# Layer 2's graph: each group of gathered edges waits for the gathers of two groups behind it

## The chip, the cores and the metric

The kernel runs on one core of one Trainium2 chip. The metric is the device time of one execution in microseconds (us). A core has five engines that run side by side, each through a queue of instructions of its own: TensorE (PE in the profile; its weight loads are PEld), VectorE (DVE), ScalarE (ACT), GpSimd (POOL) and SyncE (SP). An engine takes its queue in order. An instruction that has to wait for another engine or for a DMA holds up everything behind it in its queue.

## What is computed

The network has four layers over 4608 tokens (2 images of 48 x 48) of 256 channels: a bidirectional selective scan, linear attention with a convolution, attention followed by a graph-routed mixture of experts, and sigmoid attention followed by a second mixture of experts. The change lies in the graph of layer 2, which scores each token for four experts by attention over 1048576 edges. The core of the reference:

```python
h = (x_flat @ W_gat).reshape(M, HEADS, NUM_EXPERTS)
loops = jnp.arange(M, dtype=edge_index.dtype)
src = jnp.concatenate([edge_index[0], loops])
dst = jnp.concatenate([edge_index[1], loops])
a_src = (h * att_src).sum(-1)
a_dst = (h * att_dst).sum(-1)
e = jax.nn.leaky_relu(a_src[src] + a_dst[dst], negative_slope=0.2)
e_max = jax.ops.segment_max(e, dst, num_segments=M)
ee = jnp.exp(e - e_max[dst])
denom = jax.ops.segment_sum(ee, dst, num_segments=M)
alpha = ee / (denom[dst] + 1e-16)
msg = h[src] * alpha[:, :, None]
agg = jax.ops.segment_sum(msg, dst, num_segments=M).reshape(M, HEADS * NUM_EXPERTS) + b_gat
...
for ei in range(NUM_EXPERTS):
    g = jnp.where(topk_i == ei, w, 0.0).sum(-1)
    hh = jax.nn.gelu(x @ W1[ei] + b1[ei], approximate=False)
    out = out + g[..., None] * (hh @ W2[ei] + b2[ei])
```

The drawn edges point at up to 65536 nodes, of which 4608 exist here; an index out of range is clamped for a source and dropped for a target. Nearly all edges therefore have the last node as their source.

## The kernel before

While layers 0 and 1 run, the edges are packed into sortable keys, and each partition keeps the first ones. Edges whose source is the last node only have to be counted by target. The others are few: `edges.oth` holds 64 of them for each of the 128 partitions, one column of 128 edges at a time.

`graph_scores` handles both kinds in one block between two loops with a run-time count (lines 1131 and 1402), which no instruction crosses. In it three streams of work meet:

- The counts (`count_last`): 32 groups of 32 columns. For each, DVE builds a one-hot of the low index bits (`ol`, L1103, 128 x 4096 in bf16) and one of the high bits (`oh`, L1107), and PE multiplies them in 32 small matmuls (L1109) into one accumulator. Both one-hots have two buffers.
- The pieces (`beside[1]`): four pieces of the experts' first pass, which need no graph: matmuls `ph` (L1511), Gelu on ACT (L1515), matmuls `po` (L1526), an addition on ACT (L1530). `behind_gathers` interleaves three steps of these with each count.
- The edges (`add_edges`): eight groups of eight columns. For each column POOL issues two indirect DMAs, one that gathers the source's row into `gs` (L1207) and one for the target's row into `gd` (L1211): 128 gathers, all issued ahead of the counts in the program's text, each group into buffers of its own (eight of them). Once a group's rows are there, DVE builds the high one-hot (`oh`, L1220, which needs no gather), adds the two attention terms (`e`, L1225), applies the leaky ReLU (L1226) and subtracts the bound (L1227); ACT takes the exponential (L1228); DVE forms the message rows (L1229), and for each column a low one-hot (`ol`, L1237) and the outer product of rows and high one-hot (`wide`, L1239, 128 x 720). PE multiplies these in two matmuls per column (L1243) into `fp`. The tiles `e`, `rows` and the edges' `oh` have two buffers, `ol` and `wide` four.

The order in each engine's queue is not the order of the text. When the program is built, a scheduler plays it through with durations of its own: whenever an engine is free in that plan, it gets the instruction that comes first in the text among those whose operands are ready and whose buffers are free. The queues that come out are then fixed. The text has the counts and pieces ahead of the groups of edges, so a group's instruction gets onto DVE among the counts only where the plan finds DVE free. On the chip each instruction waits, by semaphores, for what it really needs.

After the block, layer 2 goes on with further pieces on PE, while DVE turns `acc` into the gate values `g`; then the late pieces and layer 3 follow.

Of the kernel before, what the change touches and what calls it, by code (L numbers as in the profile page):

```python
# [98 lines left out]
def bc(ap, shape, axis):  # L99

    return ap.unsqueeze(axis).to_broadcast(shape)
# [1070 lines left out]
def decode(nc, wp, bits, sidx, didx):  # L1172

    nc.vector.tensor_scalar(sidx, bits, 13, 0x1FFF, ALU.logical_shift_right, ALU.bitwise_and)
    nc.vector.tensor_scalar(sidx, sidx, -1.0, float(T - 1), ALU.mult, ALU.add)
    none = wp.tile(list(bits.shape), F32, tag="none", name="none")
    nc.vector.tensor_scalar(none, bits, 0.0, float(T), ALU.is_equal, ALU.mult)
    nc.vector.tensor_single_scalar(didx, bits, 0x1FFF, ALU.bitwise_and)
    nc.vector.tensor_tensor(didx, didx, none, ALU.add)


def add_edges(E, pools, keys, t_src, t_dst, lo_row, hi_row, fp, beside=None):


    nc = E.nc
    H, X, F, HI = 4, 4, 20, NT
    GQ = 8
    ip, cp = pools
    n = keys.shape[1]
    bits = keys.bitcast(I32)  # L1190
    sidx = ip.tile([P, n], I32, tag="sidx", name="sidx")
    didx = ip.tile([P, n], I32, tag="didx", name="didx")
    decode(nc, ip, bits, sidx, didx)
    part_i = ip.tile([P, n], I32, tag="part_i", name="part_i")
    lo = ip.tile([P, n], F32, tag="lo", name="lo")
    hi = ip.tile([P, n], F32, tag="hi", name="hi")
    nc.vector.tensor_single_scalar(part_i, didx, P - 1, ALU.bitwise_and)
    nc.vector.tensor_copy(lo, part_i)
    nc.vector.tensor_single_scalar(part_i, didx, 7, ALU.logical_shift_right)
    nc.vector.tensor_copy(hi, part_i)  # L1200
    got = []
    for q in range(n // GQ):
        gs = cp.tile([P, GQ, F], F32, tag="gs", name="gs")
        gd = cp.tile([P, GQ, 2 * H], F32, tag="gd", name="gd")
        for j in range(GQ):
            o = q * GQ + j
            nc.gpsimd.indirect_dma_start(  # L1207
                out=gs[:, j, :], out_offset=None, in_=t_src[:, :],
                in_offset=bass.IndirectOffsetOnAxis(ap=sidx[:, o : o + 1], axis=0),
            )  # L1210
            nc.gpsimd.indirect_dma_start(  # L1211
                out=gd[:, j, :], out_offset=None, in_=t_dst[:, :],
                in_offset=bass.IndirectOffsetOnAxis(ap=didx[:, o : o + 1], axis=0),
            )
        got.append((gs, gd))
    if beside is not None:
        beside()
    for q, (gs, gd) in enumerate(got):
        oh = cp.tile([P, GQ, HI], F32, tag="oh", name="oh", bufs=2)
        nc.vector.tensor_tensor(  # L1220
            oh, bc(hi[:, q * GQ : (q + 1) * GQ], [P, GQ, HI], 2), bc(hi_row, [P, GQ, HI], 1), ALU.is_equal
        )
        e = cp.tile([P, GQ, H], F32, tag="e", name="e", bufs=2)
        rows = cp.tile([P, GQ, F], F32, tag="rows", name="rows", bufs=2)
        nc.vector.tensor_tensor(e, gs[:, :, 0:H], gd[:, :, 0:H], ALU.add)  # L1225
        nc.vector.scalar_tensor_tensor(e, e, 0.2, e, ALU.mult, ALU.max)  # L1226
        nc.vector.tensor_tensor(e, e, gd[:, :, H:], ALU.subtract)  # L1227
        nc.scalar.activation(rows[:, :, H * X :], e, AF.Exp)  # L1228
        nc.vector.tensor_tensor(  # L1229
            rows[:, :, : H * X].rearrange("p i (h e) -> p i h e", h=H),  # L1230
            gs[:, :, H:].rearrange("p i (h e) -> p i h e", h=H),
            bc(rows[:, :, H * X :], [P, GQ, H, X], 3), ALU.mult,
        )
        for j in range(GQ):
            o = q * GQ + j
            ol = cp.tile([P, P], F32, tag="ol", name="ol", bufs=4)
            nc.vector.tensor_scalar(ol, lo_row, lo[:, o : o + 1], None, ALU.is_equal)  # L1237
            wide = cp.tile([P, HI, F], F32, tag="wide", name="wide", bufs=4)
            nc.vector.tensor_tensor(  # L1239
                wide, bc(oh[:, j, :], [P, HI, F], 2), bc(rows[:, j, :], [P, HI, F], 1), ALU.mult  # L1240
            )
            for z in range(2):
                nc.tensor.matmul(  # L1243
                    fp[z], lhsT=ol,
                    rhs=wide[:, z * HI // 2 : (z + 1) * HI // 2, :].rearrange("p i f -> p (i f)"),
                    start=o == 0, stop=o == n - 1,
                )


def graph_scores(E, xn, g, edges, beside, n_beside):  # L1250
# [8 lines left out]
    nc, tc, p = E.nc, E.tc, E.p  # L1259
    H, X, F, HI = 4, 4, 20, NT  # L1260
    DUMMY = T

    with ExitStack() as ctx:
        keep = ctx.enter_context(tc.tile_pool(name="gkeep", bufs=1))
        acc = keep.tile([P, HI, F], F32, name="acc")
        t_src = E.dram.tile([T, F], F32, name="t_src")
        t_dst = E.dram.tile([T + 1, 2 * H], F32, name="t_dst")
        lo_row = edges.lo_row
        hi_row = keep.tile([P, HI], F32, name="hi_row")
# [115 lines left out]
        with (  # L1385
            tc.tile_pool(name="goi", bufs=1) as ip,
            tc.tile_pool(name="goc", bufs=8) as cp,
            tc.tile_pool(name="gops", bufs=1, space=PSUM) as ps,
        ):
            fp = [ps.tile([P, HI // 2 * F], F32, name=f"fp{z}") for z in range(2)]  # L1390
            add_edges(E, (ip, cp), edges.oth, t_src, t_dst, lo_row, hi_row, fp, behind_gathers)
            for z in range(2):
                nc.vector.tensor_tensor(halves[z], halves[z], fp[z], ALU.add)

# [2 lines left out]
        with (  # L1397
            tc.tile_pool(name="gloop", bufs=1) as ip,
            tc.tile_pool(name="gcol", bufs=2) as cp,
            tc.tile_pool(name="gps", bufs=1, space=PSUM) as ps,  # L1400
        ):
            with tc.For_i(0, n_rounds, 1):
                rest = ip.tile([P, edges.NR], F32, tag="rest", name="rest")
                nc.sync.dma_start(rest, edges.rest_d[:, :])
                k8 = ip.tile([P, NP * 8], F32, tag="k8", name="k8")
                for j in range(NP):
                    part = rest[:, j * 1024 : (j + 1) * 1024]
                    nc.vector.max(k8[:, j * 8 : (j + 1) * 8], part)
                    nc.vector.match_replace(part, k8[:, j * 8 : (j + 1) * 8], part, 0.0)
                nc.sync.dma_start(edges.rest_d[:, :], rest)  # L1410
                fp = [ps.tile([P, HI // 2 * F], F32, tag=f"fp{z}", name=f"fp{z}") for z in range(2)]
                add_edges(E, (ip, cp), k8, t_src, t_dst, lo_row, hi_row, fp)
                for z in range(2):
                    nc.vector.tensor_tensor(halves[z], halves[z], fp[z], ALU.add)
# [57 lines left out]
def layer2_ffn(ctx, E, edges):  # L1472
# [61 lines left out]
    def pieces(a, b):  # L1534
        for c in range(a, b):
            yield from early(c)

    graph_scores(
        E, xn, g, edges, (pieces(0, AHEAD), pieces(AHEAD, BESIDE)), (BESIDE - AHEAD) * NX * (FT + 2)
    )  # L1540
# [592 lines left out]
```

## Time and profile before

| | |
|---|---|
| Runs | 5334.69, 5338.10, 5339.48 us; median 5338.1 us |
| Profiled execution | 5298.49 us, span 5296.7 us, mean granted TensorE clock 0.964 |
| Busy share of the span | PE 90%, DVE 66%, POOL 46%, ACT 45% |
| Counts, first and last L1103 | 3531.7 and 3756.3 us from the start of the span |
| Gathers, first and last issued | 3538.7 and 3814.5 us |
| Edges' matmuls (L1243), main run | 3777.05 to 3855.5 us |

The profile is of one execution. A timeline row has the start, the duration, the engine, the line, the operation, what it writes and reads, how many instructions are merged into it, and in brackets how long the engine stood idle just before it and what ended that. A gather's row on POOL shows how long POOL worked on issuing it; the data land later. Times below are counted from the start of the span.

### The profile page before, as it was taken

To read this page: it belongs to the slowest core of one execution; us is meant where nothing else is said; L and a number is where in the kernel's file an instruction comes from. 1 tells how busy PE (TensorE), PEld (TensorE's weight loads), DVE (VectorE), ACT (ScalarE), POOL (GpSimd) and SP (SyncE) were. 2 spreads that over 40 slices of the span, in tenths; PEclk is the share of its full clock that TensorE was granted. 3 is DMA by queue.
4 is the path that set the end of the run, shared out by engine and by line. 5 is a ranking of instruction groups with operands and counts; after the bars stand their busy time and mean duration, and the time that the engine had idled before them with its cause. 6 is when DMAs were issued, how large, how long until landed. Compare 5 with 4: busy or idle time off the path is not lost. (4 is left out here: it accounts for less than half of the span.)

```text
span 5296.7 us, 47498 instructions
## 1 busy us (share of the span) xinstructions
PE 4765.0 (90%) x15282; PEld 2642.2 (50%) x15282; DVE 3472.5 (66%) x5366; ACT 2395.3 (45%) x5021; POOL 2416.0 (46%) x1323
## 2 busy tenths in 40 slices
PE   7888888888888888877999999999999999999897
PEld 3444344444444434433555555556655555555676
DVE  4999988889888878889999544546724410211344
ACT  5767766765766766762222323422133222222221
POOL 2888887788888788886000000028612100000331
PEclk8999999999999999999999999999989999999898
DMA  4454454444544344443110000111121100000422
GB/s 155 167 173 172 169 177 159 167 173 165 173 150 161 138 162 152 162 152 135 36 44 32 6 16 1 38 33 28 19 96 48 48 3 9 7 9 6 85 84 97
DMA packets 187427, 504.63 MB, mean 95 GB/s; under 512 B 33591, under 2 KB 106683, under 8 KB 186908
## 3 DMA queue, kind: packets, MB, share of 16 engines
q1 hardware_dynamic: 178460, 488.74, 26.9%
q0 software_dynamic: 8704, 12.73, 1.6%
q8 instruction: 123, 2.02, 0.2%
q14 instruction: 140, 1.15, 0.1%
HBM read 425.88 MB, written 75.51 MB: 95 GB/s over the span
## 5 line engine op out<-in xcount | busy, mean ns | idle before, releaser
L512 PE MATMUL yp<-hc,ident 128*128 128x384 f32 x3072 | 1185.8, 517 | 206.3 <-DVE hc L558 166.1
L527 POOL TENSOR_TENSOR db<-dtu,bb 128x1536 f32<-128x1536 f32 x384 | 1322.9, 3445 | 53.5 <-DVE hs L553 13.5
L512 PEld LDWEIGHTS yp<-hc,ident 128*128 128x128 f32 x3072 | 573.4, 197 | 764.5 <-DVE hc L558 317.7
L558 POOL TENSOR_TENSOR hc<-ho,cc 128x384 f32<-128x384 f32 x576 | 587.9, 1028 | 243.6 <-DVE ho L553 103.1
L558 DVE TENSOR_TENSOR hc<-hs,cc 128x384 f32<-128x384 f32 x960 | 499.9, 538 | 82.5 <-PE yp L512 81.3
L544 ACT ACTIVATE hs<-dt,negab 128x384 f32<-128x384 f32 x768 | 435.2, 581 | 94.6 <-DVE hc L558 44.1
L544 ACT ACTIVATE hs<-dt,negaf 128x384 f32<-128x384 f32 x768 | 434.5, 581 | 67.3 <-DVE hc L558 32.6
L550 DVE TENSOR_TENSOR_SCAN hs<-hs,state,db 128x384 f32<-128x384 f32 x400 | 395.3, 1008 | 33.9 <-POOL db L527 21.5
L553 DVE TENSOR_TENSOR_SCAN hs<-hs,state,db 128x384 f32<-128x384 f32 x400 | 393.3, 1005 | 34.6 <-POOL db L527 16.1
L1938 POOL DMA_INDIRECT xe<-xt_d,token x48 | 47.4, 987 | 752.5 <-issue 713.1
L311 PE MATMUL mm<-xw,w_cv 128*128 128x384 f32 x768 | 287.5, 517 | 56.6 <-ACT xs L315 17.9
L1873 PE MATMUL po<-at,xtok 128*128 128x384 f32 x864 | 329.5, 506 | 8.2 <-ACT at L1871 8.1
L1864 PE MATMUL sp<-qT,xn 128*128 128x384 f32 x864 | 317.2, 486 | 0.0
L1871 ACT ACTIVATE at<-sp 128x384 f32<-128x384 f32 x216 | 104.8, 491 | 467.2 <-PE sp L1864 467.1
L1511 PE MATMUL ph<-xn,w 128*128 128x384 f32 x768 | 288.9, 519 | 17.7 <-ACT hid L1515 6.0
L1069 POOL PARTITION_ALL_REDUCE most<-most x1 | 0.4, 381 | 629.5 <-PE tp L939 629.5
L800 PE MATMUL pf<-t,wfc 128*128 128x384 f32 x768 | 256.0, 488 | 3.5 <-ACT hid L804 2.7
L819 PE MATMUL po<-hid,wfc 128*128 128x384 f32 x768 | 253.7, 486 | 0.0
L553 DVE TENSOR_TENSOR_SCAN ho<-hs,state,db 128x384 f32<-128x384 f32 x240 | 239.2, 997 | 14.4 <-ACT hs L544 14.3
L550 DVE TENSOR_TENSOR_SCAN ho<-hs,state,db 128x384 f32<-128x384 f32 x240 | 239.0, 996 | 8.7 <-ACT hs L544 8.7
L560 ACT COPY state<-hs 128x1 f32<-128x1 f32 x800 | 117.6, 155 | 277.5 <-DVE hc L558 274.6
L1515 ACT ACTIVATE hid<-ph,vec 128x384 f32<-128x384 f32 x192 | 110.6, 581 | 292.8 <-PE ph L1511 259.2
(465 smaller groups left out, 8022.8 us busy)
## 6 DMA issues: line engine op xcount, KB each, us to landing
bb<-bcd SPq DMA_DIRECT2D x192, 768.0 KB, 4.2
cc<-bcd SPq DMA_DIRECT2D x192, 768.0 KB, 4.1
xw<-xi_d SPq DMA_DIRECT2D x24, 774.0 KB, 5.8
w<-in_m_w SPq DMA_DIRECT2D x16, 1024.0 KB, 5.8
y_d<-y SPq DMA_DIRECT2D x32, 384.0 KB, 2.3
ye<-y_d SPq DMA_DIRECT2D x32, 384.0 KB, 3.4
xi_d<-xz SPq DMA_DIRECT2D x48, 192.0 KB, 2.3
z_d<-xz SPq DMA_DIRECT2D x48, 192.0 KB, 3.2
```

Of the source, the lines that this page charges most:

```text
L311: nc.tensor.matmul(px, lhsT=w_cv[b, s][:, d * 4 + k, :], rhs=xw[:, d, o : o + W], start=k == 0, stop=k == 3,)
L512: nc.tensor.matmul(yp[d], lhsT=E.ident, rhs=hc, start=False, stop=summed[d] == NS)
L527: nc.gpsimd.tensor_tensor(db, bc(dtu[:, d, :], [P, GN, W], 1), bb, ALU.mult)
L544: nc.scalar.activation(hs, dt[:, d, :], AF.Exp, scale=nega[s][:, d * NS + n : d * NS + n + 1])
L550: nc.vector.tensor_tensor_scan(to, hs, db[:, j], init, ALU.mult, ALU.add)
L553: nc.vector.tensor_tensor_scan(to[:, ::-1], hs[:, ::-1], db[:, j, ::-1], init, ALU.mult, ALU.add)
L558: (nc.gpsimd if on_pool else nc.vector).tensor_tensor(hc, to, cc[:, j, :], ALU.mult)
L800: nc.tensor.matmul(pf, lhsT=wfc1[:, k, f * P : (f + 1) * P], rhs=t1[:, k, :], start=k == 0, stop=k == 1,)
L819: nc.tensor.matmul(po[m], lhsT=wfc2[:, f, m * P : (m + 1) * P], rhs=hid[:, i, :], start=f == 0, stop=f == 15,)
L1511: nc.tensor.matmul(ph, lhsT=w1[:, e, k, f * P : (f + 1) * P], rhs=xn[:, k, c * W : (c + 1) * W], start=k == 0, stop=k == 1,)
L1864: nc.tensor.matmul(sp, lhsT=xn[:, k, t0 + i * P : t0 + (i + 1) * P], rhs=qT[:, k, c * W : (c + 1) * W], start=k == 0, stop=k == 1,)
L1873: nc.tensor.matmul(po[m], lhsT=xtok[:, i, m * P : (m + 1) * P], rhs=at, start=i == 0, stop=i == MT - 1,)
```

## The change

Each group's `e` gets a first write ahead of its real one. It copies one column of a later group's `gd`, the last column that is gathered there, into a part of `e`, which L1225 then overwrites. The later group is the one two further on, or the last group where there is none. The value is of no use; the copy, and so everything of the group that uses `e`, has to wait for that later gather. Only the call in `graph_scores` asks for it; the second call, in the loop over further edges, keeps the default of 0 and is unchanged.

```diff
-def add_edges(E, pools, keys, t_src, t_dst, lo_row, hi_row, fp, beside=None):
+def add_edges(E, pools, keys, t_src, t_dst, lo_row, hi_row, fp, beside=None, behind=0):
...
         e = cp.tile([P, GQ, H], F32, tag="e", name="e", bufs=2)
         rows = cp.tile([P, GQ, F], F32, tag="rows", name="rows", bufs=2)
+        if behind:
+
+            later = got[min(q + behind, len(got) - 1)][1]
+            nc.vector.tensor_copy(e[:, GQ - 1, H - 1 :], later[:, GQ - 1, 0:1])
         nc.vector.tensor_tensor(e, gs[:, :, 0:H], gd[:, :, 0:H], ALU.add)
         nc.vector.scalar_tensor_tensor(e, e, 0.2, e, ALU.mult, ALU.max)
...
-            add_edges(E, (ip, cp), edges.oth, t_src, t_dst, lo_row, hi_row, fp, behind_gathers)
+            add_edges(E, (ip, cp), edges.oth, t_src, t_dst, lo_row, hi_row, fp, behind_gathers, 2)
```

## The prediction

> **What bounds the kernel now.** I read the page first, for the engine that fills the span, then the timelines of VectorE (DVE), GpSimd (POOL) and TensorE (PE) over the graph of layer 2, and the waits there.
>
> ```profile
> span 5296.7 us, 47498 instructions
> PE 4765.0 (90%) x15282; PEld 2642.2 (50%) x15282; DVE 3472.5 (66%) x5366; ACT 2395.3 (45%) x5021; POOL 2416.0 (46%) x1323
> ```
>
> PE is busy 90% of the span, so a microsecond counts where PE loses it. The graph's block runs from 3525 us to 3856 us. PE first does counts and expert pieces, then the edges' matmuls (L1243):
>
> ```profile
> 3672.52 5.49 PE L1511 MATMUL ph<-xn,w 128*128 128x384 f32 x8 [5.78 <-ACT hid L1515]
> ...
> 3702.61 2.19 PE L1109 MATMUL cp<-oh,ol 128*128 128x36 bf16 x32 [4.91 <-DVE oh L1107]
> ...
> 3777.05 40.70 PE L1243 MATMUL fp<-wide,ol 128*128 128x360 f32 x134
> 3818.89 36.57 PE L1243 MATMUL fp<-wide,ol 128*128 128x360 f32 x120 [1.15 <-DVE wide L1239]
> 3855.30 1.45 PE L1511 MATMUL ph<-xn,w 128*128 128x384 f32 x4
> ```
>
> In 3603 to 3855 PE waits three times: 5.78 us for ACT, 4.91 us for a count's one-hot on DVE, 1.15 us for the last group. From 3777.05 the 64 edge columns run back to back for 78.25 us, 9.78 us a group. Behind them PE goes straight on (L1511), so the whole kernel moves by what the end of L1243 moves. The cause of the waits is in DVE's queue:
>
> ```profile
> 3628.92 0.45 DVE L1220 TENSOR_TENSOR oh<-hi,hi_row 128x288 f32<-128x288 f32 x1
> 3629.29 0.19 DVE L1225 TENSOR_TENSOR e<-gs,gd 128x32 f32<-128x32 f32 x1
> ...
> 3659.57 0.19 DVE L1225 TENSOR_TENSOR e<-gs,gd 128x32 f32<-128x32 f32 x1
> 3669.79 0.19 DVE L1225 TENSOR_TENSOR e<-gs,gd 128x32 f32<-128x32 f32 x1 [10.03 <-DMA gd<-t_dst,didx]
> ...
> 3680.44 0.18 DVE L1227 TENSOR_TENSOR e<-e,gd 128x32 f32<-128x32 f32 x1
> 3696.91 0.19 DVE L1225 TENSOR_TENSOR e<-gs,gd 128x32 f32<-128x32 f32 x1 [16.28 <-DMA gd<-t_dst,didx]
> ...
> 3817.63 0.19 DVE L1225 TENSOR_TENSOR e<-gs,gd 128x32 f32<-128x32 f32 x1 [3.25 <-DMA gd<-t_dst,didx]
> ```
>
> L1225 is a group's first use of its gathers. Groups 0 to 3 stand between the counts (L1103, 32 of them): group 0 behind count 16, groups 1 and 2 behind count 20, group 3 behind count 22; groups 4 to 7 come after the counts. I call these slots 16, 20 and 22. Groups 2 and 3 come before their gathers have landed, and the queue stands 10.03 and 16.28 us. The queue's order was fixed at build, by a plan that thought those gathers done. ACT stands in the same way, since its exp (L1228) is queued ahead of the pieces' Gelu:
>
> ```profile
> 3670.35 0.23 ACT L1228 ACTIVATE rows<-e 128x32 f32<-128x32 f32 x1 [9.04 <-DVE e L1227]
> ```
>
> The reader should see that these are the waits behind PE's 5.78 and 4.91 us. POOL says when gathers are done:
>
> ```profile
> 3559.48 0.94 POOL L1207 DMA_INDIRECT gs<-t_src,sidx  x1 [0.30 <-issue]
> 3560.73 4.37 POOL L1211 DMA_INDIRECT gd<-t_dst,didx  x1 [0.30 <-issue]
> ...
> 3662.47 0.94 POOL L1211 DMA_INDIRECT gd<-t_dst,didx  x1 [0.30 <-issue]
> ...
> 3814.49 0.94 POOL L1211 DMA_INDIRECT gd<-t_dst,didx  x1 [0.30 <-issue]
> ```
>
> A gather is 0.94 us and 0.30 us to the next, 1.25 us. One issued under a count's L1103 (4.42 us) lasts as long as that. Group 2's 48 gathers were issued 129.7 us after the first one (3538.7), with 19 counts in between: (129.7 - 48 x 1.25)/19 = 3.66 us per count. Group 3's 64 took 156.7 us with 21 counts: 3.65. So n gathers with k counts take 1.25n + 3.65k, and the last of them has landed 1.5 to 2.2 us later (3695.44 to 3696.91, 3815.43 to 3817.63); I take 2.2.
>
> **The change part by part.** It removes nothing and moves no DMA; POOL's and SP's queues keep their order. It adds eight copies of 128x1 on DVE. The nearest row is the 128x1 scalar operation at L924, 145 ns: 8 x 0.15 = 1.2 us at most. The four among the edge columns lie under PE: there DVE needs about 1.02 us a column (3824.72 to 3825.73) and PE 1.22. The four among the counts (0.6 us) stand beside the waits below. If that cover were gone, all eight cost 1.2 us, 0.02%.
>
> What counts is the copy's operand. Group q's copy waits for the last gather of group q+2 (of group 7 from q = 5 on), on the chip as well as in the plan. Behind it in DVE's queue stand the group's e and the next counts; ACT's exp waits for e and holds the Gelus; PE waits for both.
>
> *Where the copies stand.* Before cannot show this slot, so I bound it. The plan put a group's e where it thought the gathers done and DVE free. Had it thought all gathers slow, groups 2 and 3 would stand later than they do. Group 3 in slot 22 means: 64 gathers planned within the time to slot 22, on the trace 131.7 us without the 10.03 us stall, at most 2.06 us each. Slot 16 lies at 90.2 us, slot 20 at 119.2. The copy of group 0 (48 gathers) keeps slot 16 up to 1.88 us a gather, group 1's (64) keeps slot 20 up to 1.86, group 2's (80) up to 1.49, group 3's (96) keeps slot 22 up to 1.37. At the trace's own unblocked 1.25 us all four keep their slots, and I take that. This uses the trace's clock for the plan's; a plan that is faster throughout keeps the ratios. The other end, all copies behind the counts, is a rival below.
>
> *The stalls, all slots kept.* Slot 16: group 2's gathers are out after 48 x 1.25 + 15 x 3.65 = 114.8 us, landed at 3655.7; DVE stands 26 us where it stood none. Slot 20: group 4, 80 x 1.25 + 19 x 3.65 = 169.4, landed at 3710.3; DVE, back here at about 3682, stands some 28 us, of which 10.03 were there. Slot 22: group 5, 96 x 1.25 + 21 x 3.65 = 196.7, landed at 3737.6 against 3696.9 before. So count 23 starts 40.7 us late. Before, PE took up that count at 3702.61 after waiting for it; it has no slack, and the ten counts left with their pieces follow in full: 40.7 us on PE. Between the stalls PE has room for the 51 us of its work from 3638 to 3703, with a few us to spare. Less 1.15 us, since all gathers are in when the edge columns start at 3818.
>
> *The clock.* After the 5.78 us wait eight matmuls took 5.49 us where eight take 2.81 (3632.22), 2.7 us lost, and the granted clock (third column from the end) fell:
>
> ```profile
> 3600.00:3650.00 50.00, 50.00 (x335) 34.74 (x334) 39.22 (x27) 14.71 (x24) 43.91 (x21) 1.00 0.13 36
> 3650.00:3700.00 50.00, 41.91 (x249) 27.72 (x247) 22.76 (x21) 12.17 (x20) 41.17 (x30) 0.90 0.12 27
> ```
>
> TensorE: Matmul & The Clock Gate of the Trainium skill, Part 1, has PE fall to half rate after an idle window of about 3.4 us, and warm after as long busy: 1.7 us lost per restart. It speaks against the change: three long waits instead of two make one more restart, +1.7 us by the rule and +2.7 us by the trace, which I take. Sum: 40.7 - 1.15 + 2.7 = +42 us.
>
> *A rule that would turn the sum.* DMA: Bandwidth & Descriptors of the Trainium skill, SWDGE vs HWDGE vs iDMA, has VectorE lock GpSimd out of descriptor writing during its 2-port performance mode. L1103 shows no doubled rate (4096 elements in 4.42 us, 1.08 ns each; the f32 product L1239 takes 901 ns for 720). By that rule alone no count would slow a gather: group 2 would land at 3538.7 + 60 + 2.2 = 3601, group 5 at 3661, each ahead of its slot, and the change would be free. The gathers of 4.4 us and the stalls of 10.03 and 16.28 us say otherwise, so the trace's 3.65 us per count decides.
>
> The profiled execution took 5298.49 us (span 5296.7), 0.7% under the median of the runs, 5338.1; the difference is carried over: 5298.5 + 42 = 5340.5 there, 5380 on the median.
>
> **The rivals.** *Half of it:* the plan's gathers are slower than 1.37 to 1.49 us, and only some copies leave their slots. With group 4's gathers the last awaited among the counts, at slot 22: 80 x 1.25 + 21 x 3.65 + 2.2 = 178.9, at 3717.6, +20.7 us, with the clock about +22: 5360. For it: the plan's durations are not in the trace. Against: 1.25 us is.
>
> *The copies slip behind the counts.* Then no stall is left among the counts, PE gains 5.78 + 4.91 and the slow restarts 2.7 + 2.0 (twelve matmuls at 3704.62 took 6.11 us, else 4.10), 15.4 us, and starts the edge columns at 3762. But the gathers still end by POOL's pace, at 3817.6, and groups 5 to 7 all wait for that: about 3 us to the first matmul, then 3 x 9.78, end at 3850 against 3855.3. That is -5 us, 5333: not slower, and within what can be told from no change. It decides from a planned pace above 1.88 us a gather, with group 3 held under 2.06: a narrow window, unless the plan weighs things I do not see.
>
> *The change does nothing:* if the plan's slots for groups 0 to 3 already lay behind those gathers on the chip, eight copies would be all, +1 us. The waits of 10.03 and 16.28 us for a group's own gathers speak against it.
>
> **How the numbers follow.** A measurement of this kernel tells about 0.2% (10.7 us) from no change. All slots kept 0.60 (+36 to +54 us); half 0.18 (+11 to +36); behind the counts or nothing 0.16 (-15 to +10), of which 0.05 beyond -10.7 us should the gathers end earlier too; worse than +54, by PE starved between the stalls, 0.06. Faster 0.05, same 0.11, slower 0.84. The range goes from +2 to +54 us: 5340 to 5392.
>
> **What would show it.** In the profile after: L1225 or its copy waits for gd by some 70 us in total instead of 29.6; a stall of about 26 us behind count 16; count 23 at about 3738; L1243 from about 3818 without a wait for gathers, ended at about 3897; the POOL gathers done before it starts, at about 3814; the work behind unchanged. Wrong if the copies stand after the last L1103, or if PE's idle time in the block falls.

## The result, and the profile after

Over 20 runs each the changed kernel took 5347.46 us (5337.10 to 5365.56) and the kernel before 5338.85 us (5333.25 to 5346.61): a ratio of 1.0016 [1.0009, 1.0022], 8.6 us slower. The prediction had 42 us. Its sign was right and its size five times too large. The main reason is a wait of the kernel before that its profile did not show: on a chip where before does not have that wait, the same change cost 40 us.

The page of the changed kernel (5337.10 us, the lowest of its 20 runs) opens with:

```profile
span 5335.3 us, 47503 instructions
PE 4749.5 (89%) x15282; PEld 2631.2 (49%) x15282; DVE 3473.2 (65%) x5374; ACT 2394.0 (45%) x5021; POOL 2418.7 (45%) x1323
```

DVE has eight instructions more (5374 against 5366), the copies. The timeline of DVE shows the four that stand among the counts (start, duration, engine and line, tiles; in brackets the idle time before and what ended it). Lines of `add_edges` have moved: the copy is L1229, `e` L1230, the exp L1233, the edges' matmul L1248:

```profile
3644.68 0.15 DVE L1229 COPY e<-gd 128x1 f32<-128x1 f32 x1 [26.15 <-DMA gd<-t_dst,didx]
...
3683.52 0.15 DVE L1229 COPY e<-gd 128x1 f32<-128x1 f32 x1 [10.57 <-DMA gd<-t_dst,didx]
3703.60 0.15 DVE L1229 COPY e<-gd 128x1 f32<-128x1 f32 x1 [19.93 <-DMA gd<-t_dst,didx]
...
3731.19 0.15 DVE L1229 COPY e<-gd 128x1 f32<-128x1 f32 x1 [15.75 <-DMA gd<-t_dst,didx]
```

The copies kept slots 16, 20 (two of them) and 22, and wait 72.4 us for gathers, where before waited 26.3 us among the counts. ACT's exp is held as foreseen, PE loses two long waits to it (this trace gives only "issue" for them; `after_third`, below, names ACT), and the edge columns begin at 3818 without a pause:

```profile
3705.16 0.23 ACT L1233 ACTIVATE rows<-e 128x32 f32<-128x32 f32 x1 [30.11 <-issue]
```

```profile
3648.05 5.43 PE L1516 MATMUL ph<-xn,w 128*128 128x384 f32 x8 [21.82 <-issue]
...
3707.33 4.81 PE L1516 MATMUL ph<-xn,w 128*128 128x384 f32 x8 [26.85 <-issue]
...
3818.23 77.00 PE L1248 MATMUL fp<-wide,ol 128*128 128x360 f32 x254
```

POOL's last gather was issued at 3802.99, ahead of them:

```profile
3802.99 0.95 POOL L1212 DMA_INDIRECT gd<-t_dst,didx  x1 [0.30 <-issue]
```

In kind this is what the prediction described. That the edge columns begin at 3818, as it had it, is chance: the block itself began 12.0 us earlier here (first L1103 at 3519.70 for 3531.66) and took 12 us more than forecast to get there. Against the profile shown of before the block grew by 52 us, but the runs did not. The open question is what before does in those runs.

### The profile page after: what moved, and what is told of

The parts are those of the page before. It is cut to its first block, busy times and chain, and to the rows that moved or that the text cites. A ratio compares the mean times of both kernels' runs of the same rounds, so it can differ in the third digit from the quotient of the medians.

```text
span 5335.3 us, 47503 instructions
## 1 busy us (share of the span) xinstructions
PE 4749.5 (89%) x15282; PEld 2631.2 (49%) x15282; DVE 3473.2 (65%) x5374; ACT 2394.0 (45%) x5021; POOL 2418.7 (45%) x1323
## 3 DMA queue, kind: packets, MB, share of 16 engines
q14 instruction: 140, 1.15, 0.1%
```

## A second profile of before has a wait that the first had not

`before_again` is the kernel before, unchanged, profiled and timed again, on one chip together with three others. It took 5342.03 us, and its profile has a span of 5345.7 us, 49 us over the first. PE after the counts, in the second profile:

```profile
3777.39 1.52 PE L1511 MATMUL ph<-xn,w 128*128 128x384 f32 x4
...
3781.82 0.89 PE L1526 MATMUL po<-hid,w 128*128 128x384 f32 x2 [0.70 <-issue]
3816.23 4.95 PE L1526 MATMUL po<-hid,w 128*128 128x384 f32 x10 [33.52 <-ACT hid L1515]
3821.02 77.00 PE L1243 MATMUL fp<-wide,ol 128*128 128x360 f32 x254
```

PE stands 33.52 us for ACT. ACT and DVE in turn both stand, and both go on at the same moment:

```profile
3776.12 0.58 ACT L1515 ACTIVATE hid<-ph,vec 128x384 f32<-128x384 f32 x1 [0.84 <-PE ph L1511]
3815.60 0.58 ACT L1515 ACTIVATE hid<-ph,vec 128x384 f32<-128x384 f32 x1 [38.89 <-remote]
```

```profile
3766.49 0.75 DVE L1107 TENSOR_TENSOR oh<-hi,ids 128x1152 bf16<-128x1152 bf16 x1
3815.54 0.20 DVE L1114 COPY cnt<-cp 128x36 f32<-128x36 f32 x1 [48.29 <-remote]
```

"remote" is a semaphore event whose sender the profile could not name. Both instructions wait for PE: the copy for the last count's matmuls, the Gelu for the `ph` issued at 3777.39. By the records PE's signalling matmuls started between 3777.32 and 3782.22; the trace has their four semaphore events at 3815.51, 3815.57, 3815.63 and 3815.68, far closer together than the matmuls were. This reads as finished work that was reported 33 to 38 us late; the profile models the ends of matmuls, but the starts are on record, and DVE and ACT did stand until the events came. The same copy in the first profile of before:

```profile
3770.75 0.20 DVE L1114 COPY cnt<-cp 128x36 f32<-128x36 f32 x1 [9.39 <-PE cp L1109]
```

The stretch from 3778 to 3816 us makes the difference plain (columns: width, busy us of PE, PEld, DVE, ACT, POOL, granted clock, DMA share, GB/s). First the second profile, then the first:

```profile
3778.00:3816.00 38.00, 3.24 (x9) 1.24 (x7) 0.43 (x2) 0.40 (x1) 24.30 (x26) 0.59 0.15 5
```

```profile
3778.00:3816.00 38.00, 38.00 (x127) 23.90 (x126) 35.30 (x77) 2.05 (x5) 29.33 (x27) 1.00 0.18 16
```

In the one almost only POOL works, at its gathers; in the other PE is busy throughout. The runs fall into two kinds by that, and since all runs of one chip were of one kind, they are called kinds of chip here. On the "late" kind PE's signals come late and before takes 5338 to 5345 us: the chip of this profile, and by their times the runs of the table and the 20 runs above. On the "prompt" kind (the first profile, and all four chips that later experiments fell on) not one of some 13,000 signals of PE, DVE and ACT in a trace is more than 1 us late, and before takes 5291 to 5298 us. The traces differ in one more way: each late one, the profile after included, lacks 48 to 72 of these signals' events altogether, and no prompt one lacks any. A wait whose event is missing shows as "issue". Each ratio below is to before on the same chip.

The block by stretches, in us, from the first L1103 to the last one, on to the main run of edge matmuls, and that run:

| kernel | chip | counts | to the edge matmuls | edge matmuls | sum |
|---|---|---|---|---|---|
| before, first profile | prompt | 224.6 | 20.8 | 78.4 | 323.8 |
| after (`after_third`) | prompt | 269.2 | 20.8 | 77.0 | 367.0 |
| before (`before_again`) | late | 232.7 | 58.9 | 77.0 | 368.6 |
| after (profile after) | late | 277.7 | 20.8 | 77.0 | 375.5 |
| after (`after_again`) | late | 274.9 | 20.8 | 77.0 | 372.7 |

On a prompt chip the change adds 43.2 us to the block, on a late one 6.9 us, or 4.1 us by `after_again`, which ran on the same chip as `before_again`. It puts 42 to 45 us into the counts on either kind; on a late chip it gets 38 us back, since the wait that before has behind its counts is not met. Each row is one execution. The rest of an execution varies too (the block of these five begins between 3519.7 and 3531.7 us), so kernels are compared by the medians of their runs.

## The experiments

**The same kernels again, and the parts of the change, on a late chip** (before 5344.73 us there). `before_again` and `after_again` are the two kernels. `own_group` keeps the eight copies but lets each read its own group:

```diff
-            later = got[min(q + behind, len(got) - 1)][1]
+            later = got[q][1]
```

`behind_counts` makes the first write of `e` read the counts' result, so that every group stands behind all counts (against before, with `edges.cnt` handed in as `behind`):

```diff
+        if behind is not None:
+
+            nc.vector.tensor_copy(e[:, GQ - 1, H - 1 :], behind[:, 0:1])
```

> The kernel before, unchanged, to see what one profile stands for. In the first profile the graph's block (first L1103 to the end of the L1243 run) takes 323.6 us of an execution of 5298 us, 40 us under the median of the runs (5338.9). Theory A, the block itself varies: this profile has a block of some 355 to 365 us, with longer waits in it, in an execution near 5338 us. Theory B, the block is steady and another part varies: block 322 to 327 us again, and the 40 us lie ahead of it or behind it.

> The changed kernel, unchanged. Its first profile has a block of 375.4 us. Both theories: block 372 to 380 us, stalls of 26, 31 and 16 us at the copies. Theory A has it 8 to 12 us slower than before in the runs, since before's block takes 365 us in them. Theory B would have it 40 to 50 us slower wherever before's other parts are as in its first profile.

> The eight copies are kept, but each reads its own group's last gather, so nothing waits for a later group. If the waits for later groups are what costs: block and time as before (within 2 us of it). If the copies themselves, or the order of the queue that they bring, cost: 5 us or more slower than before.

> The first write of e reads the counts' result instead of a gather, so that all eight groups stand behind the last count in the plan and on the chip. If waits inside the counts are the cost and POOL's gathers the only other bound: no wait for a gather among the counts, L1243 starts about 15 us earlier than in before's first profile relative to the first L1103, and the block ends 5 us earlier, at most 7. If PE is bound elsewhere: the block is as long as before or longer, since the groups' first steps are no longer beside the counts.

| kernel | median us | ratio to before |
|---|---|---|
| before_again | 5342.03 | 0.9998 [0.9990, 1.0006] |
| after_again | 5350.15 | 1.0012 [1.0005, 1.0019] |
| own_group | 5347.55 | 1.0009 [1.0000, 1.0017] |
| behind_counts | 5343.66 | 1.0001 [0.9993, 1.0009] |

The result is repeated, and the block of before differs between its two profiles (368.6 us for 323.8), as theory A had it. By the medians `after_again` is 5.4 us slower, where 8 to 12 were expected, and `own_group` 2.8 us, where at most 2 were; the intervals leave room for both. The clearest case is `behind_counts`: no copy waits for a gather among the counts, so the last count's L1103 starts at 3746.2, and still the edge matmuls begin where they do in the other kernels. PE in `own_group` and then in `behind_counts`:

```profile
3808.26 6.29 PE L1531 MATMUL po<-hid,w 128*128 128x384 f32 x10 [27.99 <-ACT hid L1520]
3814.39 15.89 PE L1248 MATMUL fp<-wide,ol 128*128 128x360 f32 x52
```

```profile
3814.32 6.02 PE L1530 MATMUL po<-hid,w 128*128 128x384 f32 x10 [47.68 <-ACT hid L1519]
3820.17 10.15 PE L1247 MATMUL fp<-wide,ol 128*128 128x360 f32 x33
```

What ends earlier among the counts is waited away at their end. DVE is let go 5.6, 5.0 and 3.6 us after POOL's last gather has been issued (in `before_again` 3815.5 after 3809.9, the end of the row below; in `own_group` 3807.6 after 3802.5; in `behind_counts` 3810.1 after 3806.5), which suggested that the late signals wait for the end of POOL's run of gathers.

```profile
3808.97 0.95 POOL L1211 DMA_INDIRECT gd<-t_dst,didx  x1 [0.30 <-issue]
```

The profile after, from a late chip too, limits both this and the rival of a hold at a fixed place in the program. PE's signals from 3795 on are prompt there, though POOL issues gathers until 3803.9; and the copy that stood 48.29 us in `before_again` waits no longer than on a prompt chip:

```profile
3811.93 0.20 DVE L1114 COPY cnt<-cp 128x36 f32<-128x36 f32 x1 [9.39 <-PE cp L1109]
```

By this one trace neither a run of gathers nor this place in the program holds the signals by itself.

**Gathers left out, put late, or spaced.** `short_before` and `short_after` are the two kernels without the gathers of groups 6 and 7, which then work on the rows of groups 4 and 5:

```diff
     for q in range(n // GQ):
+        if beside is not None and q > 5:
+            got.append(got[q - 2])
+            continue
```

`late_two` issues the gathers of those groups behind the counts, with indices that DVE copies only once the counts are done:

```diff
+        for t2, t in ((s2, sidx), (d2, didx)):
+            nc.vector.tensor_copy(t2[:, 0:1], after[:, 0:1])
+            nc.vector.tensor_copy(t2, t[:, n - last * GQ :])
+        for q in range(last):
+            gather(q, s2, d2, q * GQ)
```

`spaced` puts a memset after every second gather of groups 5 to 7:

```diff
+            if beside is not None and q > 4:
+                nc.gpsimd.memset(gap, 0.0)
```

> The kernel before, with the gathers of the last two of the eight groups left out: those groups are worked on with the rows of the two groups ahead of them, so 32 of 128 indirect DMAs are missing and everything else is in its place. Theory A: in a usual execution of the kernel before, PE's last signals of the counts come through only once POOL's run of gathers is over (in the repeated profile of before PE had issued count 23's last matmul at 3777.30, but the signal came at 3815.50, 5.6 us after the last gather was issued), and this wait is what the change fills. With 32 gathers of 1.25 us fewer the run ends some 40 us earlier, at about 3770, no wait is left, L1243's run begins at 3783 to 3788 in place of 3821, and the time falls by 33 to 38 us, to about 5306 (ratio 0.993). Rival B: the signals are held by something that has nothing to do with the gathers (a fetch of code at a fixed place in the program): the wait stays at 35 to 48 us and the time at 5340 to 5345.

> The changed kernel with the same gathers left out. Theory A: the four waits of the copies among the counts stand (groups 2 to 5 are gathered as before), the counts end at about 3812 and L1243's counterpart begins at about 3819 as in the changed kernel; the time stays at 5345 to 5350. Against the kernel before with the same gathers left out it is then slower by 35 to 44 us: the cost that the prediction put on the waits, which the full kernels hide. If the waits themselves are cheap (rival: work moves into them), it is slower than its partner by under 15 us.

> The kernel before, with the gathers of the last two groups issued after the counts: their indices are copied by DVE behind the counts' result, so POOL's run has a gap between group 5 and group 6. Nothing is left out. Theory A1: PE's signals are held only while an unbroken run of gathers goes and DVE stands; the run of groups 0 to 5 ends near 3770, the signals come at once, L1243's run begins near 3785 and the gathers of groups 6 and 7 (about 42 us) go beside its first 58 us, as gathers go beside L1243 in the first profile of before: 5305 to 5312. Theory A2: any run of gathers holds PE's signals, whatever DVE does: the run of the last two groups, from about 3779 to 3820, holds L1243's run as well, and the time is 5340 to 5350. Rival B (a fetch at a fixed place): 5340 to 5345 with the wait where it was.

> The kernel before, with a POOL memset of 128x1024 elements (about 1.2 us) after every second gather of groups 5 to 7. Nothing is left out. POOL's run of gathers has 24 gaps and ends some 25 to 30 us later, near 3838. Theory A2: PE's signals are held until the run is over, whatever the gaps: L1243's run begins near 3845 and the time is 5362 to 5370. Theory A1 (an unbroken run is what holds them): the signals come in the first gap, L1243's run begins near 3785 to 3790, and the time falls to 5305 to 5315. Rival B: L1243's run begins where it did, 5340 to 5345.

(What the first of these calls count 23, with its last matmul at 3777.30, is the last count, the 32nd.) This chip was a prompt one, with before at 5291.10 us, so the question put to a late chip got no answer, and another one did:

| kernel | median us | ratio to before |
|---|---|---|
| short_before | 5287.87 | 0.9993 [0.9985, 1.0002] |
| short_after | 5332.67 | 1.0080 [1.0066, 1.0093] |
| late_two | 5295.56 | 1.0008 [0.9999, 1.0016] |
| spaced | 5309.89 | 1.0040 [1.0026, 1.0053] |

With the wait after the counts absent, the change's waits show in full: `short_after` takes 44.8 us more than `short_before`, where 35 to 44 were expected. `spaced` is slower by 19 us, as the gathers of the last group now end behind PE's need, and DVE waits for them:

```profile
3827.50 0.19 DVE L1228 TENSOR_TENSOR e<-gs,gd 128x32 f32<-128x32 f32 x1 [18.46 <-DMA gd<-t_dst,didx]
```

That leaving out or moving gathers gains no more than 3 us here fits: on a prompt chip PE goes from the counts straight to the edge matmuls, and there is no wait to take away.

**The whole change on a prompt chip, and the four again.**

> The changed kernel again. The kernel before has taken about 5341 us on some chips and 5291 us on another, on which none of PE's signals came late. Theory C (chips are of two kinds, and on the quick kind before has no wait after the counts): where before takes about 5291 here, the changed kernel takes 5330 to 5336, slower by 38 to 45 us (ratio 1.0075 to 1.0085), as the prediction's sum has it; where before takes about 5340, it is slower by 5 to 10 us (1.001 to 1.002), as measured already. Rival (the difference was one of the missing gathers alone): slower by 5 to 10 us on either kind.

> The kernel before without the gathers of the last two groups, on another chip. Where before takes about 5340 us: theory A (PE's signals wait for the end of POOL's run of gathers) has 5303 to 5310, ratio 0.993 to 0.994; a hold at a fixed place in the program has no difference. Where before takes about 5291: 5288 again, ratio 0.999 to 1.000.

> The kernel before with the last two groups' gathers issued after the counts, nothing left out, on another chip. Where before takes about 5340 us: theory A1 (an unbroken run of gathers while DVE stands holds PE's signals) has 5303 to 5315; theory A2 (any run of gathers holds them) 5340 to 5350. Where before takes about 5291: 5291 to 5297 again.

> The kernel before with a POOL memset after every second gather of groups 5 to 7, nothing left out, on another chip. Where before takes about 5340 us: theory A2 (held until the run is over) has L1243 begin near 3845 and 5362 to 5372; theory A1 (the gaps let the signals through) has L1243 begin at 3785 to 3795 and 5310 to 5325 (on the quick chip, where nothing is held, this kernel took 5310). Where before takes about 5291: 5310 again.

A prompt chip again, before at 5293.16 us. `after_third`, the changed kernel in full, took 5333.58 us: a ratio of 1.0080 [1.0066, 1.0094], 40.4 us slower, within the 38 to 45 expected. The rival, that leaving out gathers had made the difference, falls: nothing is left out here. `short_before_2` 0.9985 [0.9978, 0.9992], `late_two_2` 1.0004 [0.9996, 1.0012], `spaced_2` 1.0039 [1.0026, 1.0053] repeat the runs above. PE, DVE's copies and the count behind the last of them, and the same two stretches as in the prediction, of `after_third`:

```profile
3647.26 5.16 PE L1516 MATMUL ph<-xn,w 128*128 128x384 f32 x8 [21.91 <-ACT hid L1520]
...
3706.34 4.64 PE L1516 MATMUL ph<-xn,w 128*128 128x384 f32 x8 [26.92 <-ACT hid L1520]
...
3736.35 2.19 PE L1109 MATMUL cp<-oh,ol 128*128 128x36 bf16 x32 [5.74 <-DVE oh L1107]
3738.37 5.25 PE L1516 MATMUL ph<-xn,w 128*128 128x384 f32 x12
...
3809.94 77.00 PE L1248 MATMUL fp<-wide,ol 128*128 128x360 f32 x254
```

```profile
3643.81 0.15 DVE L1229 COPY e<-gd 128x1 f32<-128x1 f32 x1 [26.16 <-DMA gd<-t_dst,didx]
...
3682.43 0.15 DVE L1229 COPY e<-gd 128x1 f32<-128x1 f32 x1 [10.55 <-DMA gd<-t_dst,didx]
3702.60 0.15 DVE L1229 COPY e<-gd 128x1 f32<-128x1 f32 x1 [20.02 <-DMA gd<-t_dst,didx]
...
3730.22 0.15 DVE L1229 COPY e<-gd 128x1 f32<-128x1 f32 x1 [15.78 <-DMA gd<-t_dst,didx]
...
3731.21 4.42 DVE L1103 TENSOR_TENSOR ol<-lo,lo_ids 128x4096 bf16<-128x4096 bf16 x1
```

```profile
3600.00:3650.00 50.00, 28.09 (x186) 19.30 (x186) 19.51 (x17) 8.50 (x13) 41.16 (x30) 0.78 0.09 20
3650.00:3700.00 50.00, 29.42 (x191) 20.01 (x189) 19.36 (x14) 7.09 (x11) 41.31 (x29) 0.81 0.10 20
```

The copies wait as long as in the profile after (72.5 us for 72.4), and PE's waits are nearly the same; here nothing gives them back.

**The gathers once more, and the copies alone.** For a late chip `short_before` and `late_two` were run twice more, with expectations like those of their second run (as `short_before_3`, `late_two_3`, `short_before_4`, `late_two_4`): 0.9987 [0.9981, 0.9994] and 1.0005 [0.9996, 1.0014] with before at 5297.80 us, then 0.9998 [0.9989, 1.0007] and 1.0002 [0.9993, 1.0011] with before at 5292.21 us. Prompt chips both, as was the last:

> The kernel before without the gathers of the last two groups, a last time. Where before takes about 5340 us: theory A (PE's signals wait for the end of POOL's run of gathers, which ends 40 us earlier here) has 5303 to 5310; the rival (a hold at a fixed place in the program, whatever POOL does) has 5338 to 5345. Where before takes about 5291: 5285 to 5292 again.

> The changed kernel with each copy reading its own group's rows: the eight copies and their order stay, and nothing waits for a later group. Where before takes about 5291 us: if the waits make the change's 40 us, this kernel is within 4 us of before (ratio 0.9995 to 1.0008); if the copies or the shifted order make a part of them, it is slower by that part, 5 us or more. Where before takes about 5340: slower by 0 to 8 us, as measured.

With before at 5293.21 us, `short_before_5` had 0.9989 [0.9983, 0.9996], and `own_group_2` took 5298.29 us, 1.0009 [1.0002, 1.0016]. These 5.1 us are more than the 4 that it was to stay within if the waits make all of the cost, so by its own expectation the copies or the shifted order cost something, though the interval (1 to 8 us) reaches below 4. In its trace the gathers take 279.8 us from the first issue to the last (3530.31 to 3810.14), where they took 275.8 in the first profile of before (3538.67 to 3814.49), and PE's pause for the last group is longer (3.40 us where it was 1.15), with slower matmuls behind it (39.59 us for 36.57):

```profile
3814.49 39.59 PE L1248 MATMUL fp<-wide,ol 128*128 128x360 f32 x120 [3.40 <-DVE wide L1244]
```

By these two profiles most of that cost lies where the edge matmuls wait for the last group. The full change does not have that part (77.00 us without a pause), so by far the most of its 40 us comes from the waits among the counts. Why the gathers took longer is not shown.

## Why the prediction was right or wrong

- *What bounds it, and where the copies stand:* right. All four copies kept slots 16, 20, 20 and 22.
- *The stalls:* right, each slightly low. 26 us were expected at slot 16 and 26.16 measured, some 28 us at slot 20 and 30.57 (10.55 + 20.02), and slot 22 another 15.78. Count 23 stood 165.8 us behind the first count (3697.47 in the first profile of before) and stands 211.3 us behind it in `after_third`: 45.5 us late for 40.7.
- *The clock:* mis-sized. From count 23 to the last count 0.9 us were won where 2.7 were to be lost. The granted clock did fall, to 0.78 and 0.81 in the two stretches. But the restarts cost little more than before's. The eight matmuls behind the two long waits took 5.16 and 4.64 us for 2.81 unhurt, 2.4 and 1.8 us lost. Behind the third wait, 5.74 us, the count matmuls took their usual 2.19 us, and the twelve `ph` matmuls after them 5.25 for 4.10, 1.2 us lost. The three restarts lost 5.3 us, where before's two had lost 4.7 (2.7 and 2.0): 0.6 us more. The prediction's 1.7 us per restart "by the rule" is an estimate, half of the window of 3.4 us in TensorE: Matmul & The Clock Gate of the Trainium skill, Part 1; measured here are 1.2 to 2.7 us.
- *The end of the gathers:* right. The edge matmuls start with all gathers in; 1.41 us won for 1.15.
- *The sum:* 45.5 - 0.9 - 1.4 = 43.2 us in the block for the predicted 42, and 40.4 us over the runs of a prompt chip. That it comes so close is partly luck, since stalls that were set 4.8 us too small and a clock term 3.6 us too large cancel.
- *The step that failed:* "the difference is carried over". The profiled execution of before stood 39.6 us under the median of the runs, and the prediction took this as a constant that has nothing to do with the change. In the second profile of before most of it is a wait in this very block, behind the counts, that costs 38 us and in which PE, DVE and ACT stood while POOL went on with its gathers. With it, "it has no slack, and the ten counts left with their pieces follow in full" no longer holds: a count that is late by 45 us uses up 38 us in which PE would have waited. On such chips the stalls cost 6.9 and 4.1 us by the blocks, 8.6 and, repeated, 5.4 us by the runs (medians of 5350.15 and 5344.73).
- *The rivals:* none was this one. "The copies slip behind the counts" was tried by `behind_counts`, on the late chip: the prediction had 5 us faster, and no difference was measured; on a prompt chip it was not run.

Left open: why PE's signals come late on some chips, and what POOL's gathers have to do with it. The times of release speak for a part of theirs, the prompt signals of the profile after against the gathers as the sole cause; the kernels that would have shown it ran on prompt chips only, five times `short_before`, four times `late_two` and twice `spaced`. A fetch of code is not shown as the cause: an instruction fetch of 8 KB starts 1.7 and 1.1 us ahead of the release in `before_again` and `own_group`, but in `behind_counts` the next one starts at 3810.38, when DVE was already let go. Whether the missing events have the same cause as the late ones is open too. That the chip makes the difference is the plain reading of one chip with the wait and four without; something else that differed between those runs is not excluded, and the record names no chip for the first profile, the runs of the table and the 20 runs. No version run here beats before: `short_before` leaves work out.

## What to carry to other kernels

A profiled execution that lies outside the spread of the timed runs (here 39.6 us under runs that lay within 5 us) is not those runs with a constant added. The missing time sits in some place, and if a wait could sit behind the change, the change may fall into it: give that case a chance of its own. And before a stall is charged in full, ask whether the stalled engines will wait at the end of the stage anyway: here 38 us of such a wait took up most of 45 us of stalls.

## What was not expected of the hardware

The same kernel took 5342 us on one chip and 5291 to 5298 us on four others, at nearly the same mean granted clock (0.962 and 0.964 in its two profiles), and most of it is one place where PE's signals arrived 33 to 38 us after the matmuls' own records, while POOL issued indirect DMAs at its even 1.25 us and almost nothing else ran. Among the counts the late chip lost 8 us more (232.7 us for 224.6), with several of the counts' own signals some 1.2 us late (a count's last matmul ended at 3755.17, its event came at 3756.40). Of the 13,269 signals of PE, DVE and ACT the late trace of before lacks 51 events, the prompt one none.
